# Order of the last products in the odd channels of the core stage, and the count of two kinds of tiles

## The chip, the cores and the metric

The kernel runs on one NeuronCore of a Trainium2 chip. The metric is the device time of one execution in microseconds. Five engines work side by side from queues of their own: PE (matrix products, with its weight loads shown apart as PEld), DVE (vector), ACT (scalar), POOL (GpSimd) and SP (which here issues the transfers). An instruction that needs another engine's result waits at the head of its own queue, and what stands behind it waits too.

## What is computed

Two layers on a pair tensor x of 384 x 384 tokens with 128 channels. Only the first one bears on the change:

```python
z = _layernorm(x, norm_g, norm_b)
left = (z @ Wl + bl) * sigmoid(z @ Wlg + blg)
right = (z @ Wr + br) * sigmoid(z @ Wrg + brg)
core = einsum('bikh,bjkh->bijh', left, right)     # for each of 128 channels h: 384x384 times 384x384
zo = _layernorm(core, onorm_g, onorm_b) @ Wout + bout
x = x + sigmoid(x @ Wg + bg) * zo
```

The second layer makes left, right and gate from the new x, multiplies left by the row sum of right and by the gate, goes through one more matrix and normalises over the channels.

## The kernel before, in words

There are three stages, one after the other. **Stage 1** (0 to about 1010 us) reads x, makes `left` and `right` and writes them to `lr_d` in device memory, ordered by channel. **Stage 2** (about 1010 to 1746 us) makes the core, channel by channel, and writes it to `core_d`. **Stage 3** (to the end) reads the core back row by row and does everything else. The change lies in stage 2.

Stage 2 is the loop of line 664 over channels h, 126 of them, and a short ending for the last two (lines 720 to 769). For each channel `load_h` (L92) brings left and right together into a tile `lrh` of three that take turns. ACT copies the right half to a tile `rr` of its own (`apart`, L632), of the pool `p2r` with three buffers: three copies for each channel, one for each block of 128 summands. The result goes to a tile `ct` of the pool `p2out` with two buffers, from which SP stores it (`store_core`, L645). Line 718 asks for the load of channel h+3 at the end of channel h, when its tile is free again.

Channels go in pairs, and the two passes of a pair differ.

**Even channel** (lines 668 to 682): `plain` computes the product in nine block products of 384 columns, three for each of three banks of `pc`. Beside it POOL prepares the odd channel: `left_sums` (L618, four small sums into `ss`) and `right_sums2` (L623, L627, L628, into `tt`), both in the tile `arena` but for one piece.

**Odd channel** (lines 684 to 716): the upper two thirds of the product are made with seven products per two-by-two block, instead of eight, in the manner of Strassen and Winograd. The block row 2 is plain: three products of 384 columns into bank `b4`. Eleven products of 192 columns go into banks `b0` to `b3`. DVE combines them in eight additions (`add`, L651). Their order on PE and DVE is written out by hand, since every instruction is given through `seq`, which keeps the order of the program on its engine. The part that matters:

```python
add(base, b1, one)            # L702
add(more2, b2, base)          # L703
add(base, b3, base)           # L704
add(least, b2, base)          # L705: the fourth sum, the last reader of b2
product(b0, ...); product(b0, ...); product(b1, ...); product(b1, ...)   # L706 to L709
product(b2, block(h, 2, 1), B[2][1])                                    # L710
product(b3, ...); product(b3, ...)                                      # L711, L712
```

A bank is read by DVE in the first four additions and is then written by PE once more, in the products of L706 to L712, so each of those products has to wait for the last addition that read its bank. `b0` is read by ACT (L692), `b1` by L702, `b3` by L704, and `b2` by L703 and L705. All products have one helper line, L648: in the profile those of the even pass have the name `pc` and those of the odd one the name `b`. Each product of float32 shows as two weight loads and two matmuls.

Also on the way: `squares` (L635, ACT) and `add_sum` and `add_squares` (L638 and L642, DVE) gather the sums for the normalisation; `stay` (L610, POOL) copies the part of left and right that never left the chip; at the end `fill` (L585 to L592, POOL) does for channel 127 what ACT does for the others.

Of the kernel before, what the change touches and what calls it, by code (L numbers as in the profile page):

```python
# [19 lines left out]
def triangle_then_gated_row_kernel(ctx: ExitStack, tc: tile.TileContext, a: dict, out: bass.AP):  # L20
# [35 lines left out]
    def seq(ins):  # L56

        return tc.keep_in_program_order(ins)
# [21 lines left out]
    with ExitStack() as ctx2:  # L80
# [4 lines left out]
        def load_h(h):  # L85

            if h < H:
                t = inp[h % 3 // 2].tile([P, NB, N, 2], F32, tag="lrh", name="lrh")
                src = lr_d[:, :, h].rearrange("g p e -> p g e")
                dst = t.rearrange("p b (g i) s -> p (b g) (i s)", i=G)  # L90
                for g in slice(0, NG), slice(NG, NB * NG - KEEP):
                    seq(nc.sync.dma_start(out=dst[:, g], in_=src[:, g]))  # L92
                loaded2[h] = t
# [465 lines left out]
            seq(nc.vector.scalar_tensor_tensor(r, r, -0.5, ve, ALU.mult, ALU.mult))  # L559
            seq(nc.vector.scalar_tensor_tensor(r, r, 1.5, m, ALU.add, ALU.mult))  # L560

        with tc.tile_pool(name="p2r", bufs=3, side="right", reuse_waits="tile") as rrp, \
             tc.tile_pool(name="p2more", bufs=1, side="right", reuse_waits="tile") as more, \
             tc.tile_pool(name="p2out", bufs=2, side="right", reuse_waits="tile") as op, \
             tc.tile_pool(name="p2st", bufs=1, side="right", reuse_waits="tile") as stp:
            csum = spool.tile([P, NB, N], F32, name="csum")
            csq = spool.tile([P, NB, N], F32, name="csq")
# [5 lines left out]
            right = {}  # L573
# [23 lines left out]
            js = slice(0, J), slice(J, N)  # L597
            one, base, more2, least = (arena[:, n, j] for n in (2, 2 * NB) for j in js)
# [5 lines left out]
            def block(h, k, i):  # L604
                return loaded2[h][:, k, i * P:(i + 1) * P, 0]

            def stay(h):

                for (kb, ig), lrt in kept.items():
                    seq(nc.gpsimd.tensor_copy(loaded2[h][:, kb, ig * G:(ig + 1) * G], lrt[:, h]))  # L610

            def left_sums(h):

                for n, x, y, op in ((0, block(h, 0, 1), block(h, 0, 0), ALU.subtract),
                                    (1, block(h, 0, 1), block(h, 1, 1), ALU.add),
                                    (2, ss[1], block(h, 0, 0), ALU.subtract),
                                    (3, block(h, 1, 0), ss[2], ALU.subtract)):
                    seq(nc.gpsimd.tensor_tensor(ss[n], x, y, op))  # L618

            def right_sums2(h):  # L620

                rr = right[h]
                seq(nc.gpsimd.tensor_tensor(  # L623
                    tt[:, 0:2], rr[:, 0, js[1]].unsqueeze(1).to_broadcast([P, 2, J]),
                    rr.rearrange("p b n -> p (b n)").rearrange("p (a m) -> p a m", a=2)[:, :, js[0]], ALU.subtract,
                ))
                seq(nc.gpsimd.tensor_tensor(tt[:, 2], rr[:, 0, js[0]], tt[:, 1], ALU.subtract))  # L627
                seq(nc.gpsimd.tensor_tensor(tt[:, 3], rr[:, 1, js[0]], tt[:, 2], ALU.subtract))  # L628

            def apart(h, k):  # L630

                seq(nc.scalar.copy(right[h][:, k], loaded2[h][:, k, :, 1]))  # L632

            def squares(h):
                seq(nc.scalar.activation(sq, cts[h], AF.Square))  # L635

            def add_sum(h, c=None):
                seq(nc.vector.tensor_add(csum, c or cts[h], csum))  # L638

            def add_squares(h):  # L640
                if h >= 0:
                    seq(nc.vector.tensor_add(csq, csq, sq))  # L642

            def store_core(h, queue=nc.sync):
                seq(queue.dma_start(out=core_d[:, h, :].rearrange("(b p) j -> p b j", p=P), in_=cts[h]))  # L645

            def product(to, lhsT, rhs, start=True, stop=True):
                seq(nc.tensor.matmul(to, lhsT=lhsT, rhs=rhs, start=start, stop=stop))  # L648

            def add(out, ps, term):  # L650
                seq(nc.vector.tensor_add(out, ps, term))  # L651

            def plain(h, banks):

                for k in range(NB):
                    for i in range(NB):
                        product(banks[i], block(h, k, i), right[h][:, k], k == 0, k == NB - 1)

            fill(0)
            with tc.tile_pool(name="p2mix", bufs=1, space=PSUM, reuse_waits="tile") as mps:  # L660
                pc = mps.tile([P, NB, 512], F32, name="pc")
                b0, b1, b2, b3 = (mps.tile([P, 512], F32, name="b%d" % n)[:, :J] for n in range(4))
                b4 = mps.tile([P, 512], F32, name="b4")[:, :N]
                for h in range(H - 2):
                    cts[h] = op.tile([P, NB, N], F32, tag="ct", name="ct")
                    right[h + 1] = rrp.tile([P, NB, N], F32, tag="rr", name="rr")
                    if h % 2 == 0:
                        plain(h, [pc[:, i, :N] for i in range(NB)])
                        if h > 0:
                            store_core(h - 1)  # L670
                        add_squares(h - 2)
                        stay(h + 1)
                        left_sums(h + 1)
                        for k in range(NB - 1):
                            apart(h + 1, k)
                        right_sums2(h + 1)
                        if h > 0:
                            squares(h - 1)
                            add_sum(h - 1)
                        apart(h + 1, NB - 1)  # L680
                        if h > 0:
                            add_squares(h - 1)
                    else:
                        rr, ct = right[h], cts[h]
                        B = [[rr[:, k, j] for j in js] for k in range(NB)]
                        product(b0, block(h, 0, 0), B[0][0])
                        for k in range(NB):
                            product(b4, block(h, k, 2), rr[:, k], k == 0, k == NB - 1)
                        seq(nc.scalar.copy(cts[h - 1], pc[:, :, :N]))
                        store_core(h - 1)  # L690
                        add_sum(h - 1, pc[:, :, :N])
                        seq(nc.scalar.copy(one, b0))  # L692
                        stay(h + 1)
                        for k in range(NB - 1):
                            apart(h + 1, k)
                        seq(nc.scalar.copy(ct[:, 2], b4))
                        apart(h + 1, NB - 1)
                        squares(h - 1)
                        product(b1, ss[2], tt[:, 2])
                        product(b2, ss[0], tt[:, 1])  # L700
                        product(b3, ss[1], tt[:, 0])
# [3 lines that stand above are left out]
                        add(least, b2, base)  # L705
                        product(b0, block(h, 1, 0), B[1][0], True, False)  # L706
                        product(b0, block(h, 2, 0), B[2][0], False, True)
                        product(b1, ss[3], B[1][1], True, False)
                        product(b1, block(h, 2, 0), B[2][1], False, True)  # L709
                        product(b2, block(h, 2, 1), B[2][1])  # L710
                        product(b3, block(h, 1, 1), tt[:, 3], True, False)  # L711
                        product(b3, block(h, 2, 1), B[2][0], False, True)  # L712
                        add(ct[:, 0, js[0]], b0, one)
                        add(ct[:, 0, js[1]], b1, base)
                        add(ct[:, 1, js[1]], b2, least)
                        add(ct[:, 1, js[0]], b3, more2)
                    del right[h], loaded2[h]
                    load_h(h + 3)
                store_core(h)
            with tc.tile_pool(name="p2ps", bufs=2, space=PSUM, reuse_waits="tile") as ps, \  # L720
                 tc.tile_pool(name="p2one", bufs=1, space=PSUM, reuse_waits="tile") as ps1:
                for h in range(H - 2, H):
# [19 lines left out]
                    ct = op.tile([P, NB, N], F32, tag="ct", name="ct")  # L742
# [32 lines left out]
    with ExitStack() as ctx3:  # L775
        def pool(name, bufs, **kw):
            return ctx3.enter_context(tc.tile_pool(name=name, bufs=bufs, reuse_waits="tile", **kw))
# [3 lines left out]
        wp, sp, op, up = pool("p3w", 4), pool("p3s", 4), pool("p3out", 3), pool("p3u", 18)  # L781
# [324 lines left out]
```

## Time and profile before

| what | value |
|---|---|
| median of 3 runs | 3151.19 us (3149.53 to 3152.18) |
| the profiled execution's own time | 3148.3 us |
| its span | 3146.2 us |
| granted PE clock | 0.999 |
| PE busy | 3126.9 us (99%) |
| PE idle between matmuls in 1030 to 1730 us | 0.48 us of 700 us |
| DMA share in 1030 to 1380 and 1380 to 1730 us | 0.97 and 0.96, at 286 GB/s |

The span is the time from the first instruction to the last in the one execution that was profiled, and lies 2.1 us under that execution's own time. A matmul's end is modelled in these profiles, and matmuls overlap one another, so a PE that counts as busy can still be held up: the starts of the instructions tell more than the busy time does. A view of the trace merges neighbouring instructions of one kind; "x4" at the end of a line is their number, and what stands in brackets after it is the idle time of the engine before the first of them and who ended it.

### The profile page before, as it was taken

How to read it: one execution, taken by the hardware profiler on the slowest of the kernel's cores; microseconds unless marked ns; L12 is line 12 of the kernel's file. 1: busy time of each engine (PE TensorE's matmuls, PEld its weight loads, DVE VectorE, ACT ScalarE, POOL GpSimd, SP SyncE). 2: the span in 40 equal slices, each digit the busy share in tenths (PEclk: the TensorE clock that was granted, in tenths of full speed). 3: DMA queues.
4: the chain of work that ended last, by engine and by line, in shares of the span. 5: the costliest groups of instructions: out<-in, count | busy, mean ns of one | idle time of the engine just before them, and what ended most of it. 6: DMA issues, size and time to landing. Idle time of an engine off the chain costs nothing.

```text
span 3146.2 us, 47062 instructions
## 1 busy us (share of the span) xinstructions
PE 3126.9 (99%) x11936; PEld 2208.3 (70%) x11936; DVE 2586.9 (82%) x7913; ACT 1947.3 (62%) x4196; POOL 2380.6 (76%) x3003
## 2 busy tenths in 40 slices
PE   9999999999999999999999999999999999999998
PEld 4777777777777777777777666677777777777776
DVE  8888888888886777776777888888888888888998
ACT  4444444444444555555655577677777777777776
POOL 6888888888886666656666588788888888888887
PEclk9999999999999999999999999999999999999999
DMA  4988878788883999999999865666666666666562
GB/s 153 339 302 306 323 281 339 280 324 302 302 316 99 284 287 287 284 287 286 284 288 285 289 230 209 224 225 218 223 216 221 217 222 218 219 221 220 207 216 106
DMA packets 509117, 797.58 MB, mean 254 GB/s; under 512 B 56689, under 2 KB 419569, under 8 KB 492466
## 3 DMA queue, kind: packets, MB, share of 16 engines
q1 hardware_dynamic: 507952, 793.20, 74.3%
q8 instruction: 99, 1.62, 0.2%
q14 instruction: 168, 1.38, 0.1%
q10 hardware_dynamic: 834, 1.18, 0.1%
q0 software_dynamic: 64, 0.20, 0.0%
HBM read 508.14 MB, written 286.36 MB: 253 GB/s over the span
## 4 chain that ended last, share of the span: by engine, by line
PE 98%; DVE 1%; ACT 0%; issue 0%; POOL 0%; POOLq 0%; DVEq 0%; ACTq 0%
PE pr L372 31%; PE pc L648 12%; PE b L648 11%; PE py L904 8%; PE pr L875 8%; PE pg L892 8%; PE pl L893 8%; PE pg L844 8%; PE py L905 4%; PE pt L335 0%; PE pc L732 0%; PE pq L852 0%; ACT py L939 0%; PE pb L863 0%; POOL rs L286 0%
## 5 line engine op out<-in xcount | busy, mean ns | idle before, releaser
L372 PE MATMUL pr<-wz,xc 128*128 128x512 f32 x2176 | 934.7, 592 | 0.0
L372 PEld LDWEIGHTS pr<-wz,xc 128*128 128x128 f32 x2176 | 670.5, 308 | 263.4 <-POOL xc L324 0.8
L383 ACT ACTIVATE sg<-pr,rs 128x256 f32<-128x256 f32 x1152 | 483.7, 471 | 508.1 <-ACT sg L383 354.8
L385 DVE SCALAR_TENSOR_TENSOR lr<-pr,rs,sg 128x256 f32<-128x256 f32 x1152 | 502.3, 478 | 163.9 <-ACT sg L383 158.6
L939 ACT ACTIVATE py<-py,nm,rs 128x128 f32<-128x128 f32 x1149 | 493.2, 430 | 159.2 <-DVE u L897 81.6
L904 PEld LDWEIGHTS py<-wo,u 128*128 128x128 f32 x2304 | 376.6, 191 | 97.5
L904 PE MATMUL py<-wo,u 128*128 128x128 f32 x2304 | 402.1, 275 | 0.0
L866 POOL TENSOR_TENSOR cs<-ct,rt 128x384 f32<-128x384 f32 x380 | 378.6, 997 | 8.2 <-PE pr L875 3.3
L974 POOL TENSOR_TENSOR yt<-yt,lnb 128x384 f32<-128x384 f32 x380 | 379.6, 1000 | 2.9 <-DVE yt L968 2.8
L648 PE MATMUL pc<-rr,lrh 128*128 128x384 f32 x1134 | 376.1, 486 | 1.1 <-POOL rr L591 1.1
L324 POOL TENSOR_TENSOR xc<-xc,bc 128x512 f32<-128x512 f32 x272 | 345.3, 1270 | 24.0
L286 POOL TENSOR_TENSOR rs<-nd,mhalf 128x8 f32<-128x8 f32 (+1 forms) x145 | 236.3, 1630 | 147.1 <-ACT sg L383 109.2
L919 DVE BATCH_NORM_STATS2 st<-py 128x6 f32<-128x128 f32 x1152 | 266.5, 287 | 87.8 <-PE py L905 86.0
L905 PE MATMUL py<-ident,x1T 128*128 128x128 f32 x1152 | 314.0, 273 | 0.0
L875 PE MATMUL pr<-cs,wc 128*128 128x384 f32 x768 | 313.5, 490 | 0.0
L892 PE MATMUL pg<-x1T,mat_L_conv_W_gate 128*128 128x384 f32 x768 | 310.7, 486 | 0.9 <-ACT g L895 0.9
L844 PE MATMUL pg<-xt,mat_L_conv_Wg 128*128 128x384 f32 x768 | 310.7, 487 | 0.3 <-ACT ct L758 0.2
L648 PEld LDWEIGHTS pc<-rr,lrh 128*128 128x128 f32 x1134 | 220.3, 196 | 129.1 <-POOL rr L591 1.8
L893 PE MATMUL pl<-x1T,mat_L_conv_W_left 128*128 128x384 f32 x768 | 310.5, 486 | 0.0
L618 POOL TENSOR_TENSOR arena<-lrh 128x128 f32<-128x128 f32 x126 | 110.5, 877 | 256.6 <-DMA lrh<-lr_d 211.7
L648 PE MATMUL b<-rr,lrh 128*128 128x192 f32 x1134 | 296.5, 386 | 0.5 <-DVE arena L651 0.5
L895 ACT ACTIVATE g<-pg,col_L_conv_b_gate 128x384 f32<-128x384 f32 x384 | 223.0, 581 | 103.4 <-PE pg L892 92.8
(151 smaller groups left out, 5209.3 us busy)
## 6 DMA issues: line engine op xcount, KB each, us to landing
lr_d<-lr SPq DMA_DIRECT2D x128, 1024.0 KB
lrh<-lr_d SPq DMA_DIRECT2D x128, 640.0 KB
xt<-in_x_row_dram SPq DMA_DIRECT2D x96, 768.0 KB
ct<-core_d SPq DMA_DIRECT2D x95, 768.0 KB
rt<-rstd_d SPq DMA_DIRECT2D x95, 768.0 KB
core_d<-ct SPq DMA_DIRECT2D x126, 576.0 KB
out_dram<-yt SPq DMA_DIRECT2D x94, 768.0 KB
xt<-in_x_nat_dram SPq DMA_DIRECT2D x136, 512.0 KB
```

What stands on the lines that cost most here:

```text
L372: seq(nc.tensor.matmul(pr[:, r, :], lhsT=columns[n][:, 4 * q + i, :] if n < PLAIN else columns[n][:, q, :, i], rhs=wz, start=True, stop=Tr ...
L383: seq(nc.scalar.activation(sg[r], pr[:, r, 2 * H:], AF.Sigmoid, scale=rs[r]))
L385: seq(nc.vector.scalar_tensor_tensor(t[:, :, c * XR + r0 + r, :], pr[:, r, :2 * H].rearrange("k (h s) -> k h s", s=2), rs[r], sg[r].rearra ...
L648: seq(nc.tensor.matmul(to, lhsT=lhsT, rhs=rhs, start=start, stop=stop))
L844: seq(nc.tensor.matmul(pg[:, :N], lhsT=wg0, rhs=r["xT"], start=True, stop=True))
L875: seq(nc.tensor.matmul(pr[:, :N], lhsT=wc, rhs=r["cs"], start=True, stop=True))
L892: seq(nc.tensor.matmul(pg2[:, :N], lhsT=wgate, rhs=r["x1T"], start=True, stop=True))
L893: seq(nc.tensor.matmul(pl[:, :N], lhsT=wleft, rhs=r["x1T"], start=True, stop=True))
L904: seq(nc.tensor.matmul(py[:, s], lhsT=r["u"][:, s], rhs=r["wo"], start=True, stop=False))
L905: seq(nc.tensor.matmul(py[:, s], lhsT=r["x1T"][:, s], rhs=ident, start=False, stop=True, is_transpose=True))
L939: seq(nc.scalar.activation(py[:, s], py[:, s], AF.Identity, bias=bias, scale=scale))
L974: seq(engine.tensor_tensor(yt, yt, lnbb, ALU.add))
```

## The change

In the odd pass, the product into `b2` (L710) goes behind the two into `b3` (L711, L712), and the two additions that read them at the end (L715, L716) change places in the same way. The pool `p2r` (tiles `rr`) has two buffers in place of three, and `p2out` (tiles `ct`) three in place of two; both kinds have the same size, so the two pools together take the same room. Nothing is computed otherwise.

```diff
-        with tc.tile_pool(name="p2r", bufs=3, side="right", reuse_waits="tile") as rrp, \
+        with tc.tile_pool(name="p2r", bufs=2, side="right", reuse_waits="tile") as rrp, \
              tc.tile_pool(name="p2more", bufs=1, side="right", reuse_waits="tile") as more, \
-             tc.tile_pool(name="p2out", bufs=2, side="right", reuse_waits="tile") as op, \
+             tc.tile_pool(name="p2out", bufs=3, side="right", reuse_waits="tile") as op, \
              tc.tile_pool(name="p2st", bufs=1, side="right", reuse_waits="tile") as stp:
...
                         product(b1, block(h, 2, 0), B[2][1], False, True)
-                        product(b2, block(h, 2, 1), B[2][1])
                         product(b3, block(h, 1, 1), tt[:, 3], True, False)
                         product(b3, block(h, 2, 1), B[2][0], False, True)
+                        product(b2, block(h, 2, 1), B[2][1])
                         add(ct[:, 0, js[0]], b0, one)
                         add(ct[:, 0, js[1]], b1, base)
+                        add(ct[:, 1, js[0]], b3, more2)
                         add(ct[:, 1, js[1]], b2, least)
-                        add(ct[:, 1, js[0]], b3, more2)
```

## The prediction

> **What bounds the kernel now.** I read the busy times and the chain of the page first, then the stage by windows, then the waits of the product line, then single stretches of the timeline.
>
> ```profile
> PE 3126.9 (99%) x11936; PEld 2208.3 (70%) x11936; DVE 2586.9 (82%) x7913; ACT 1947.3 (62%) x4196; POOL 2380.6 (76%) x3003
> ...
> PE 98%; DVE 1%; ACT 0%; issue 0%; POOL 0%; POOLq 0%; DVEq 0%; ACTq 0%
> ```
>
> PE is the chain almost throughout, so only what holds PE counts. But "99%" doesn't say that PE is never held: ends of matmuls are modelled. In the view of line 648:
>
> ```profile
> its engine sat idle before it (us, times) until:
>   DVE arena L651: 12.4, 65
>   POOL rr L591: 2.9, 2
>   POOL arena L627: 0.5, 2
> ```
>
> The product line waits for a DVE addition into `arena` 65 times, nearly once in each of 63 pairs of channels. The timeline of PE and of its weight loads in one pair says where:
>
> ```profile
> 1513.60 0.81 PE L648 MATMUL b<-rr,lrh 128*128 128x192 f32 x4
> 1514.25 0.49 PE L648 MATMUL b<-rr,s 128*128 128x192 f32 x2
> 1514.57 0.97 PE L648 MATMUL b<-rr,lrh 128*128 128x192 f32 x4
> 1515.38 0.49 PE L648 MATMUL b<-arena,lrh 128*128 128x192 f32 x2
> 1515.71 0.49 PE L648 MATMUL b<-rr,lrh 128*128 128x192 f32 x2
> ```
>
> ```profile
> 1514.41 0.36 PEld L648 LDWEIGHTS b<-rr,lrh 128*128 128x128 f32 x2
> 1514.95 0.31 PEld L648 LDWEIGHTS b<-rr,lrh 128*128 128x128 f32 x2 [0.17 <-DVE arena L651]
> ```
>
> The first column is the start. Four matmuls take 0.65 us from start to start (1513.60 to 1514.25), but the four from 1514.57 take 0.81: 0.16 us lost, between the second product of `b1` (L709) and that of `b2` (L710). The weight load of L710 waits for the fourth addition (L705, `least`). DVE's timeline shows its four additions:
>
> ```profile
> 1513.22 1.67 DVE L651 TENSOR_TENSOR arena<-b,arena 128x192 f32<-128x192 f32 x4
> ```
>
> They end at 1514.89, and the weight load starts at 1514.95. From all starts of the trace: a matmul of 192 columns follows another after 162.5 ns and one of 384 after 322.5, everywhere in the stage, but for two places around L710 (215 and 275 ns). That is 165 ns in each of 61 pairs; in two pairs the third and fourth additions are 350 ns late, and 515 ns are lost. A pair takes 11.48 us.
>
> **What the Trainium skill says.** PSUM — Partial Sum Buffer, "PSUM bank collisions raise a hardware error": two engines may not be on one bank at once, reads with reads included, so PE must wait for the reader of the bank. The trace agrees: L710's load starts 0.06 us after `least` ends. TensorE: Matmul & The Clock Gate, "Step-by-step: what each phase is for": matmuls stay in program order and only weight loads are pulled ahead. So PE can't pass L710, though L711 and L712 could run; the trace shows them behind it. SBUF — State Buffer, on the two separate sides of access (engine ports and DMA): DVE with two SBUF inputs and POOL lock each other out of a port pair for a whole instruction. Here L618 takes 458 ns at the least and 1456 at the median for one form; this matters for the first rival. Perfetto Trace Analysis, "Identifying the Most-Contended Engine": occupancy of 16 DMA engines is misleading; here it is 0.96 to 0.97 in this stage.
>
> **Part 1, the order of products.** Removed: L710's wait. The two `b3` products (four matmuls) come first, and `b3` was last read by the third addition (L704). In a usual pair, counted from the first `pc` matmul, L704 ends at 9.94 us and `least` at 10.34. The weight load at this place would start at 10.18 without a wait; releases take 0.05 us more. So `b3` is free 0.18 us early, and `b2`, now 4 x 162.5 = 650 ns later (10.83), 0.44 us early. Both waits go. `tt[:, 3]` (L628), which L711 needs too, is over two us earlier. Gain: 61 x 165 ns + 2 x 515 ns = 11.1 us. In the two odd pairs the third addition ends at 10.30; released at 10.35, the load is 0.17 us late. A load put off by 0.21 us (10.39 for 10.18) cost PE 0.165, so this costs some 0.12: 2 x 0.12 = 0.25 us stay. On DVE the eight additions are the same; the last one still follows PE's last product, and its bank isn't written again for six us. Nothing else is moved, no DMA among it.
>
> **Part 2, three `ct` tiles.** A `ct` waits for the store three channels back, not two. In the waits of 1030 to 1760 us:
>
> ```profile
> POOL arena L618 <- DMA lrh<-lr_d: 209.6, 97, 4.0
> ...
> ACT rr L632 <- DMA lrh<-lr_d: 106.6, 77, 3.3
> ACT ct L696 <- DMA core_d<-ct: 27.0, 33, 1.8
> ```
>
> The 27.0 us should go. Behind L696 on ACT stand the third copy to `rr`, `squares`, and the next pass's copies. PE needs the third copy for the next even pass's seventh product (after 12 matmuls of 322.5 ns, 3.9 us into it), and it is there before; nothing of the 27 us reaches PE. Worth 0; it keeps SP's late stores harmless.
>
> **Part 3, two `rr` tiles.** A wait is added: the first copy for the next odd channel must now wait until PE has read the odd channel before it. ACT in the pair shown:
>
> ```profile
> 1515.62 0.53 ACT L632 COPY rr<-lrh 128x384 f32<-128x384 f32 x1
> 1517.79 0.55 ACT L632 COPY rr<-lrh 128x384 f32<-128x384 f32 x1 [1.64 <-DMA lrh<-lr_d]
> ```
>
> The copy at 1515.62 would start when the last odd matmul ends, about 1516.25, and end by 1516.8. Queued behind it on ACT is the copy of 1517.79, which waits for its load anyway, and `squares` behind that. Cover: 1 us here, and over 0.4 in nearly every pair (second copies start at 1.25 us or later in most). PE needs the first copy 5.5 us into the even pass, POOL's L623 needs it about 5.5 us in. Without the cover it would cost ACT up to 0.6 us, still not PE. In the odd pass the copies stand behind L689, which has waited for the even pass already. Cost 0. At the end, `fill` of channel 127 now waits for channel 125's products (1734.5, not 1731.5), but its next step waits for a load until 1736.15 anyhow, with 0.7 us of small copies to do: 0. The two pools keep their room together; which tiles of stage 3 lie over which is shifted by one tile, taken as 0, at most 1 us either way.
>
> **What is late next.** The loads. DMA's share leaves 0.035 of 11.48 us. Work of 0.965 x 11.48 = 11.08 us would be 97.9% of the new pair, 24 x 322.5 + 22 x 162.5 ns = 11.315 us. It fits, barely. The odd channel's load is asked for when the even pass before it ends, so its deadline comes 165 ns sooner. On it hang L618, L623, L627, then the first product that uses `tt` (L699). From the end of L627 to that weight load there are 0.57 us in the typical pair, but 52, 53, 67 and 113 ns in four, and under 300 in seven; two already wait (0.26 us). If all shift by 165 ns, the four lose 0.11 + 0.11 + 0.10 + 0.05 = 0.4 us; by twice that (load delayed as well), seven lose 1.3. I take 1.0; bounds 0 and, if the DMA share can't rise at all, the whole 11. I take little because stretches of 0.6 us in the transfers' view of two pairs reach 366 to 381 GB/s against a mean of 286, so the share isn't a wall.
>
> **Sum.** -11.1 + 0.25 + 1.0 = -9.8 us. Against the profiled execution: 3148.3 - 9.8 = 3138.5 (span 3136.4). The median of the runs is 2.9 us above that execution: 3151.2 - 9.8 = 3141.4. That median's runs differ by 2.7 us; some 0.2% (6.3 us) is what a measurement can tell from no change.
>
> **Rivals.** *Loads take part of it* (0.14): the chain load, L618, L627, L699 stalls PE in a third or more of the pairs. For it: 209.6 us of POOL's waits are for loads, and a first L618 that starts after DVE's L642 is locked out and loses over a microsecond. Against: typical slack 0.57 us, and each stall gives the loads time again. 21 to 42 pairs at 0.17 us: 3.5 to 7 us off the 10.85 us, 3144 to 3147.5. *The wait moves* (0.07): the release for `b3` is counted at the fourth addition, or the third comes later than now; then the change doesn't do what it says and L711 waits where L710 did: 3151. For: slack is only 0.18 us. Against: in 61 pairs that addition's end varies by under 20 ns. *Two `rr` tiles bind, slower* (0.06): if the copy for the next odd channel must wait for the even pass under way (its nine products end at 6.0 us), the first two copies run from 6.0 to 7.1, L623 to 8.1, L627 to 8.7, against a weight load at 7.74: 1.0 us in 63 pairs, 63 - 11 = 52 us slower, 3203. It decides from the point where copies end after some 5.5 us. Against: the tile is taken from the channel two back, which PE has left at 0.2 us.
>
> **How the numbers follow.** Forecast 0.73, its own range 3139 to 3143.5; loads 0.14; moved wait 0.07; slower 0.06. The range 3138.5 to 3147 takes in the forecast and most of the loads' case. Faster by over 0.2% (under 3144.9): 0.73 + 0.04 = 0.77; within 0.2%: 0.10 + 0.07 = 0.17; slower 0.06.
>
> **What would show it.** Right: 162.5 ns from start to start all through the odd pass, 11.315 us for a pair, L648's idle time for DVE near 0, no wait of L696 for a store, first `rr` copies at about 0.2 us into the even pass. Wrong: waits of L648 for POOL L627 in many pairs (loads), for DVE L651 at L711 (moved), or for ACT L632 (two tiles).

## The result, and the profile after

The changed kernel takes 3137.5 us (median of 5 runs, 3136.1 to 3139.4), the kernel before 3151.1 in the same comparison (5 runs, 3149.5 to 3152.2): ratio 0.9958, 95% interval 0.9943 to 0.9972, or 13.6 us less. The forecast was 3141.4, range 3138.5 to 3147.0: the direction was right, the gain was larger than the range allowed, by 1 us. Two later comparisons gave 11.9 and 12.0 us.

The profiled execution of the changed kernel took 3139.4 us, span 3137.6. The view of line 648, in which the kernel before had waited 65 times for a DVE addition:

```profile
its engine sat idle before it (us, times) until:
  issue: 1.4, 3
  POOL arena L627: 1.0, 3
  DVE lr L385: 0.4, 1
```

The wait for `arena` from DVE's line 651 is gone. DVE's L385 and most of "issue" belong to the start of the stage; POOL's L627 will matter below. PE's timeline in one pair (first column start, then length, and the number of instructions at the end of the line):

```profile
1497.18 0.81 PE L648 MATMUL b<-rr,lrh 128*128 128x192 f32 x4
1497.83 0.49 PE L648 MATMUL b<-rr,s 128*128 128x192 f32 x2
1498.15 0.49 PE L648 MATMUL b<-rr,lrh 128*128 128x192 f32 x2
1498.48 0.49 PE L648 MATMUL b<-arena,lrh 128*128 128x192 f32 x2
1498.80 0.81 PE L648 MATMUL b<-rr,lrh 128*128 128x192 f32 x4
1499.45 4.03 PE L648 MATMUL pc<-rr,lrh 128*128 128x384 f32 x12
```

From 1497.18 to 1499.45 there are 14 matmuls in 2.27 us, 162 ns each: no gap is left. The fourth line is the first `b3` product, which now stands where the `b2` product waited. A pair takes 11.315 us from start to start, to the nanosecond what the forecast gave, where it was 11.48. And the waits of the stage (engine and line, what it waited for, us in all, times, the longest):

```profile
ACT rr L632 <- DMA lrh<-lr_d: 108.1, 86, 2.9
...
ACT rr L632 <- PE b L648: 60.1, 54, 1.4
...
POOL rr L586 <- PE b L648: 3.1, 1, 3.1
...
PEld b L648 <- POOL arena L627: 1.0, 3, 0.6
```

The copies to `rr` now wait 60.1 us for PE, the price of two tiles; the first copy of a pair starts at 0.2 us of it, as forecast, and ends at 0.75 us in nearly every pair. Nobody waits for them. The wait of L696 for a store (27.0 us before) is gone.

Below, a profiled execution is split by PE's first matmuls: stage 1 up to the first product of the core; "the pairs", from there to the first product of channel 126; and the rest. All "excess" times are sums over the starts of matmuls in the 63 pairs, each beyond 162.5 or 322.5 ns.

| us | stage 1 | the pairs | rest |
|---|---|---|---|
| before | 1010.5 | 724.0 | 1411.7 |
| after | 1012.4 | 713.6 | 1411.7 |

The pairs give 10.4 us; stage 1, which the change doesn't touch but for its end, went the other way by 1.9 in this one execution. So the trace of one execution showed less than the medians, and the question was what the rest is.

### The profile page after: what moved, and what is told of

Its sections match the earlier page's. It is cut to its first block, busy times and chain, and to the rows that moved or that the text cites. A ratio compares the mean times of both kernels' runs of the same rounds, so it can differ in the third digit from the quotient of the medians.

```text
span 3137.6 us, 47186 instructions
## 1 busy us (share of the span) xinstructions
PE 3117.4 (99%) x11936; PEld 2209.1 (70%) x11936; DVE 2581.1 (82%) x7913; ACT 1949.7 (62%) x4196; POOL 2369.4 (76%) x3003
## 4 chain that ended last, share of the span: by engine, by line
PE 98%; DVE 1%; ACT 0%; POOL 0%; issue 0%; DMA 0%; SPq 0%; POOLq 0%; DVEq 0%; ACTq 0%
PE pr L372 31%; PE pc L648 12%; PE b L648 11%; PE py L904 8%; PE pr L875 8%; PE pg L892 8%; PE pl L893 8%; PE pg L844 8%; PE py L905 4%; PE pc L732 0%; DMA stage<-in_x_nat_dram 0%; PE pq L852 0%; PE pt L335 0%; POOL rs L286 0%; DVE lr L385 0%
## 5 line engine op out<-in xcount | busy, mean ns | idle before, releaser
L385 DVE SCALAR_TENSOR_TENSOR lr<-pr,rs,sg 128x256 f32<-128x256 f32 x1152 | 501.9, 477 | 165.6 <-ACT sg L383 160.1
L632 ACT COPY rr<-lrh 128x384 f32<-128x384 f32 x378 | 205.0, 553 | 171.5 <-DMA lrh<-lr_d 108.4
L618 POOL TENSOR_TENSOR arena<-lrh 128x128 f32<-128x128 f32 x126 | 105.4, 837 | 259.4 <-DMA lrh<-lr_d 206.4
```

The lines of the kernel that those rows point to most:

```text
L385: seq(nc.vector.scalar_tensor_tensor(t[:, :, c * XR + r0 + r, :], pr[:, r, :2 * H].rearrange("k (h s) -> k h s", s=2), rs[r], sg[r].rearra ...
```

## The experiments

My theory at the start: the order of the products brings everything, the tiles nothing. The rivals: the tiles bring the 3 us that were left over; or shorter pairs can't do without the third `ct` tile. In every table, "lost before tt" is the excess at the first product that uses `tt` (L699), that is, PE waiting for POOL's L627; "late L642" counts pairs whose first addition L642 starts after 0.6 us of the pair, where 0.48 is usual.

**The kernel before and the changed one again.**

> The kernel before, unchanged, to see how far stages 1 and 3 alone differ from run to run. Theory (the whole gain is the wait of the b2 product): its 63 pairs take 724.0 us again; stage 1 lies anywhere between 1008 and 1013 us, ratio 1.000 within 0.001. Rival (the kernel after has a second gain of some 3 us outside the pairs): stage 1 and stage 3 repeat within 0.5 us here, so that a difference of 3 us means something.

> The changed kernel, unchanged, a second time. Theory: the 63 pairs take 713.6 us again, 10.4 less than before, and the ratio is 0.9967, 3140.7 for 3151.1; what went beyond that in the first measurement (13.6 us of median) was spread of stages 1 and 3. Rival (a second gain outside the pairs): 13.6 us less again, ratio 0.9957, and stage 1 or stage 3 shorter by 3 us in the trace.

Measured: the kernel before had ratio 1.0003 (0.9995 to 1.0011) to 26 other runs of itself in that comparison, whose median was 3149.21; the changed kernel 0.9963 (0.9950 to 0.9975), 3137.33 us, 11.9 us less, between the theory's 0.9967 and the rival's 0.9957. Its level is that of the first time; it is the kernel before that was 1.9 us lower here. The traces: pairs at 713.62 for the changed kernel, as expected, but 725.80 for the kernel before, not 724.0. Stage 1 was 1010.6 and 1010.3. In the view of line 648 of the kernel before, second time:

```profile
  DVE arena L651: 12.2, 65
  POOL arena L627: 4.4, 6
  POOL rr L591: 2.9, 2
```

L627 had been 0.5 us in the profile that the forecast was made from. So the kernel before has a second loss, which happened to be nearly absent in that one profile.

**One half at a time.** The order alone takes the changed kernel and gives it back the tiles:

```diff
-        with tc.tile_pool(name="p2r", bufs=2, side="right", reuse_waits="tile") as rrp, \
+        with tc.tile_pool(name="p2r", bufs=3, side="right", reuse_waits="tile") as rrp, \
-             tc.tile_pool(name="p2out", bufs=3, side="right", reuse_waits="tile") as op, \
+             tc.tile_pool(name="p2out", bufs=2, side="right", reuse_waits="tile") as op, \
```

The tiles alone are the other lines of the change: two `rr`, three `ct`, products and additions in the order of before.

> Only the products and additions change places; three rr tiles and two ct tiles as before. Theory: all of the gain, pairs at 713.6 us, ratio 0.9967; ACT again waits some 27 us for stores before L696 and no rr copy waits for PE. Rival 1 (the tiles bring a part): pairs above 715 us or a ratio 3 us worse than the full change. Rival 2 (shorter pairs need the third ct tile): stores hold ACT longer, over 40 us, and the pairs come to 717 us or more.

> Only the counts of tiles change, two rr and three ct; order of products as before. Theory: no change, pairs at 724.0 us within 0.5, ratio 1.000; the wait of L696 for stores is gone and rr copies wait some 60 us for PE instead, both off the path. Rival 1 (the tiles bring the 3 us): ratio 0.999 and a stage that is shorter by 3 us. Rival (two rr tiles cost): pairs over 725 us.

Measured: the order alone 0.9968 (0.9957 to 0.9980), 3138.95 us, 10.3 less; pairs at 714.13, L696 waits 32.7 us for stores. The tiles alone 0.9998 (0.9989 to 1.0006), 3148.30 us; pairs at 724.24, excess at the two places of L710 10.9 us (11.05 in the kernel before). So the order brings nearly all, and the full change, in the same comparison, is 1.6 us under the order alone. The traces showed where to look. In the order alone PE lost 0.8 us before `tt`, in three pairs, each with a late L642; in one of them, ACT, DVE, POOL and the weight loads:

```profile
1248.86 0.48 ACT L696 COPY ct<-b 128x384 f32<-128x384 f32 x1 [1.02 <-DMA core_d<-ct]
1249.23 0.55 ACT L632 COPY rr<-lrh 128x384 f32<-128x384 f32 x1
1249.67 1.17 ACT L635 ACTIVATE arena<-ct 128x1152 f32<-128x1152 f32 x1
```

```profile
1250.87 1.36 DVE L642 TENSOR_TENSOR csq<-csq,arena 128x1152 f32<-128x1152 f32 x1 [0.88 <-ACT arena L635]
1252.15 1.35 DVE L638 TENSOR_TENSOR csum<-ct,csum 128x1152 f32<-128x1152 f32 x1
1254.47 1.36 DVE L642 TENSOR_TENSOR csq<-csq,arena 128x1152 f32<-128x1152 f32 x1 [0.97 <-ACT arena L635]
```

```profile
1252.93 0.94 POOL L618 TENSOR_TENSOR arena<-lrh 128x128 f32<-128x128 f32 x1 [2.29 <-DMA lrh<-lr_d]
1253.95 0.46 POOL L618 TENSOR_TENSOR arena<-arena,lrh 128x128 f32<-128x128 f32 x1
1254.49 1.66 POOL L618 TENSOR_TENSOR s<-lrh,arena 128x128 f32<-128x128 f32 x1
```

```profile
1257.83 0.79 PEld L648 LDWEIGHTS b<-arena 128*128 128x128 f32 x5 [0.81 <-POOL arena L627]
```

Read it downwards. A store still holds the `ct` tile, so L696 waits 1.02 us. Behind it on ACT stands `squares` (L635), which therefore ends at 1250.84. DVE's L642 needs it and starts at 1250.87, which is 1.47 us into the pair in place of 0.48. That pushes DVE's three long additions back; the last of them, at 1254.47, coincides with the fourth L618, which takes 1.66 us where 0.46 is its time alone. In this pair the load was late too (2.29 us). L627 ends late, and the weight load of L699 waits 0.81 us. With three `ct` tiles the first link is missing. The link from DVE to POOL is the one the Trainium skill describes (SBUF — State Buffer, section "SBUF: two separate sides"): a DVE instruction with two SBUF inputs, as L642 and L638 here, and a POOL instruction that reads SBUF exclude each other, each for its whole length. The trace agrees: 1.66 us beside L642, 0.46 us alone.

**Is the link real?** Three edits of the new order. First, two tiles of each kind: only the third `ct` tile is missing.

```diff
-             tc.tile_pool(name="p2out", bufs=3, side="right", reuse_waits="tile") as op, \
+             tc.tile_pool(name="p2out", bufs=2, side="right", reuse_waits="tile") as op, \
```

> The new order with two rr tiles and two ct tiles, so that of the change only the third ct tile is missing. Theory now (two rr tiles cost nothing; the third ct tile takes away some stalls at the first product with tt, since no store then delays squares on ACT and with it the addition L642 on DVE, which shuts POOL out): as the new order alone, pairs at 713.8 to 715 us, L696 waits for stores 25 to 40 us, PE waits for L627 in 3 to 10 pairs, ratio 0.9968. Rival (the two rr tiles bring what the full change has beyond the order): pairs under 713.7 us and hardly a wait for L627.

Measured: 0.9967 (0.9955 to 0.9980), 3138.09 us; pairs at 714.61, L696 waits 25.3 us for stores, 1.3 us lost before `tt` in two pairs, L642 late in both (1.69 and 1.90 us). Weight loads wait five times for L627; PE loses time in two of these pairs. As the theory said; two `rr` tiles don't take this loss away. The time tells less than the profile: 3138.09 us is 11.9 us under the kernel before of this comparison, as far as the full change came in two others.

Second, with three `rr` and two `ct` tiles, `squares` ahead of the copy that waits for the store:

```diff
+                        squares(h - 1)
                         seq(nc.scalar.copy(ct[:, 2], b4))
                         apart(h + 1, NB - 1)
-                        squares(h - 1)
```

> The new order, three rr and two ct tiles, and in the odd pass squares goes ahead of the copy L696 on ACT, so that a store which holds L696 no longer holds squares. Theory (the link from the store to PE is squares, L642, POOL): L696 still waits for stores, but L642 starts at 0.48 us of nearly every even pass, and the stalls for L627 are as with three ct tiles, 0 to 2 pairs and under 0.4 us lost; ratio 0.9963 to 0.9965. Rival (stores delay the loads themselves, or the link is the copies to rr): waits for L627 in 3 to 10 pairs as with the order alone, ratio 0.9968.

Measured: 0.9968 (0.9955 to 0.9980), 3139.50 us; pairs at 714.31, 0.8 us lost before `tt` in two pairs. L642 was late in one pair of 62, against 15 and 6 in two profiles of the order alone, so that link was cut nearly as meant. But the expectation failed: the ratio is the rival's, and the loss was not smaller than with the order alone (0.8, and 0.4 in its second profile). One of the two pairs that lost time had a late load instead, with the second L618 at 3.76 us; the other is the one with the late L642 (1.24 us). The copy of L696, line 697 here, waited for stores only three times, 2.8 us in all: `squares` covers most of that wait. With two such pairs the run decides nothing.

Third, the opposite: the changed kernel with L642 late in every pair. No load, store or product moves; what moves is `squares` on ACT, and with it the second copy to `rr`, which now stands behind it.

```diff
-                        add_squares(h - 2)
                         stay(h + 1)
                         left_sums(h + 1)
-                        for k in range(NB - 1):
-                            apart(h + 1, k)
+                        apart(h + 1, 0)
+                        if h > 0:
+                            squares(h - 2)
+                        add_squares(h - 2)
+                        apart(h + 1, 1)
...
                         apart(h + 1, NB - 1)
-                        squares(h - 1)
                         product(b1, ss[2], tt[:, 2])
...
                     if h == H - 2:
+                        squares(h - 2)
                         add_squares(h - 2)
```

> The changed kernel with one thing made late on purpose: the squares of the even channel go behind the first rr copy of the next even pass on ACT (which waits for PE until 0.2 us), so that the addition L642 starts at 1.95 us of every even pass instead of 0.48, as it did in single pairs behind a store. No load, store or product is moved. Theory (a late L642 is what shuts POOL out and stalls the first product with tt): waits of PE for L627 in most of the 63 pairs, 0.3 to 0.8 us each, pairs at 730 to 765 us, ratio 1.001 to 1.012. Rival (the stalls come from late loads, and L642 is late beside them): a handful of waits as before, pairs at 713.5 to 716 us, ratio 0.9963 to 0.997.

Measured: 1.0027 (1.0018 to 1.0036), 3160.09 us, by the ratios some 20 us over the changed kernel. L642 starts at 1.89 us at the median, pairs take 733.5 us, and of 20.6 us excess 20.2 lie before `tt`. In the waits of the stage:

```profile
DVE csq L642 <- ACT arena L635: 87.0, 63, 2.4
...
PEld b L648 <- POOL arena L627: 39.9, 59, 1.9
```

A late L642 alone is enough: 59 weight loads wait for L627, where the changed kernel has 1 to 6 in its four profiles. The second copy to `rr` is not what holds POOL: in each of the 63 pairs L623 starts at the end of the fourth L618 and at least 1.2 us after that copy. In the pair from 1105.68 us on, the last three L618 take 1.56, 1.45 and 1.46 us. This is the link from L642 to PE, shown by itself. Its size came out at the low end of what I expected, 0.3 us a pair, because POOL gets in between DVE's additions where the load is early.

**How often it happens by itself.** Four more profiles.

> The new order alone a second time, for its stalls: the first time three pairs lost 0.8 us in all before the first product with tt. Theory (late L642 behind stores): again 2 to 5 such pairs, each with L642 at over 1.1 us of the pair, pairs at 713.8 to 715 us. Rival (chance of the loads alone): such pairs have L642 at 0.48 us.

> The kernel before a third time, for its pairs: 724.0 and 725.8 us so far. Theory (stalls of L627 behind a held store come and go): 724 to 726 us, with 0 to 2 us lost at the first product with tt. Rival (the 725.8 was an exception): 724.0 again within 0.2.

> The changed kernel a third time, for its pairs: 713.57 and 713.62 so far. Theory (with three ct tiles no store holds squares, L642 is never late): 713.4 to 713.8 us and L642 at 0.48 us in all pairs. Rival (chance): over 714 us, as with the order alone.

> The tiles alone a second time, for its pairs: 724.2 us so far, with 0.4 us lost at the first product with tt in one pair. Theory: 723.9 to 724.4 us, L642 never late. Rival (chance): 725 us or more.

Measured: pairs at 713.75 (order alone), 727.98 (before), 715.09 (after), 723.95 (tiles alone). The single times of these runs were 3139.45, 3158.04, 3140.17 and 3148.62 us; the second of them has a stage 1 of 1015.6 us, 5 more than the first profile of the same kernel, and its 4.1 us lost before `tt` are beyond the 0 to 2 that I expected. My expectation for the changed kernel failed too: 1.8 us were lost before `tt`, with L642 at 0.48 us in all pairs. The loads alone did it, the second L618 starting at 4.80 us in one pair and 3.97 in the other. The one for the order alone held half: of its two pairs one had a late L642. All profiles of the unedited halves, with the three that follow under "The halves once more":

| profiles | lost before tt, us | pairs held up by over 20 ns | of these with late L642 |
|---|---|---|---|
| two ct: before (3), order alone (3), two and two (1) | 0, 1.9, 4.1; 0.8, 0.4, 2.4; 1.3 | 20 | 18 |
| three ct: after (4), tiles alone (3) | 0.3, 0.3, 1.8, 0.6; 0.4, 0.1, 0.4 | 10 | 0 |

Means: 1.6 and 0.5 us. One of the 18 is a pair of the kernel before with L642 at 0.69 us and the second L618 as late as 4.63 us: there the load is the cause, of 1.15 of that profile's 1.9 us.

In most of these pairs the load is late beside L642, so the rival that loads do it all has to be answered. In 16 of the 18 the second L618 starts 1.26 to 1.41 us after L642, and ACT's second copy, 0.11 us before it, shows that the load has just landed. The pairs of these 14 profiles can be compared at equal loads, by the start of that copy, which waits for its load in all the pairs counted below. With L642 on time, no pair is held in which the copy starts before 3.4 us; the twelve that are held have it at 3.43 to 4.69 us. With L642 at 1.2 us or later and the copy at 2.5 to 3.2 us, all 13 pairs are held, 5.3 us in all, and of the 136 pairs with L642 on time and the copy in the same stretch not one. So the loss has two sources, a late L642 and a late load, and the third `ct` tile takes the first away: L642 is late in 5 to 15 pairs of a profile with two `ct` tiles, and in none with three (the first pair, where nothing has been stored yet, left out). The size of it, about 1 us by the means, is less certain: one execution, long as a whole (3158.04 us), gives 4.1 us of it, and without it the means are 0.6 us apart.

**A lost wait made longer.** The order of before, but with the `b2` product earlier, ahead of the two into `b1`:

```diff
                         product(b0, block(h, 2, 0), B[2][0], False, True)
+                        product(b2, block(h, 2, 1), B[2][1])
                         product(b1, ss[3], B[1][1], True, False)
                         product(b1, block(h, 2, 0), B[2][1], False, True)
-                        product(b2, block(h, 2, 1), B[2][1])
```

> The order of before, but with the b2 product moved the other way, ahead of the two into b1. Its weight load would then be due at 9.53 us of the pair, and the fourth addition still releases the bank at 10.39: 0.86 us late where the kernel before is 0.21 us late for 0.165 us of PE. Theory (PE is held by this release and by nothing else here, and a late load costs its lateness less 0.04 us): 0.82 us lost in each pair, 0.65 more than before, pairs at 724.0 + 41 = 765 us, ratio 1.013. Rival (the lost 0.165 us was a fixed price of one waiting instruction, not the lateness): 0.165 us again, ratio 1.000.

Measured: 1.0130 (1.0114 to 1.0145), 3190.27 us; pairs at 764.8, 0.81 us lost in a usual pair. Both numbers are the theory's. It is the lateness of the release that PE pays, and the place in the order that sets it. The two additions that change places with the products were not tested apart; L642, which stands behind them, starts at 0.48 us of a usual pair before and after.

**The halves once more, on one chip.**

> The changed kernel timed a third time. Theory (the order is worth 10.7 us, the third ct tile about 1 more, and the 13.6 us of the first measurement held some 2 us of a high level of the kernel before): 11 to 12.5 us less, ratio 0.9961 to 0.9965. Rival (the first measurement was the usual size): 13.6 us again, ratio 0.9957.

> The new order alone, timed on the same chip as the full change. Theory: some 1 us above the full change, 0.5 to 1.6, as in the first comparison (3138.95 against 3137.33), stalls for L627 with L642 late in 2 to 5 pairs. Rival (the tiles are worth nothing): within 0.4 us of the full change.

> The tiles alone, timed on the same chip. Theory: 0.5 to 2 us under the kernel before, ratio 0.9993 to 0.9998, L642 never late. Rival (worth nothing): ratio 1.000 or over.

Measured: the full change 0.9961 (0.9948 to 0.9973), 3137.43 us, 12.0 less than 3149.46; the order alone 0.9967 (0.9955 to 0.9979), 3139.78 us; the tiles alone 0.9998 (0.9989 to 1.0006), 3148.76 us. The full change is 2.35 us under the order alone (1.6 the first time), more than the 0.5 to 1.6 expected; the tiles alone are 0.7 under the kernel before (0.9 the first time). The ratio of the tiles alone doesn't clear its interval, so their size rests on the traces. Pairs: 713.87, 715.68 and 724.32.

These traces showed a second effect of the tiles, at the passage from stage 1 to stage 2, where `fill` makes the first `rr`. POOL's timeline of the kernel before:

```profile
1009.57 0.87 POOL L591 COPY rr<-lrh 128x768 f32<-128x768 f32 x1 [17.86 <-PE pr L372]
```

and what the view of line 591 says of the changed kernel:

```profile
L591 POOL COPY rr<-lrh x2: 882/1446/2009, 1005.2 to 1729.1; 128x768 f32<-128x768 f32 x2
...
  PE pr L372: 10.8, 1
```

The copy waits for the last reader of what lay at that place in stage 1. It starts 0.75 us after the start of stage 1's last matmul in all eight profiles with three `rr` tiles, and 6.2 us before it in all nine with two. The first product of the core follows that matmul after 1.67 us in the eight (1.665 to 1.675), and after 0.96 to 1.05 in the nine: 0.7 us, which is not in the numbers for the pairs. That the place of the first tile moved is read from the code; that the gain goes with the count of `rr` tiles is shown.

## Why the prediction was right in kind and too small

The step that failed is in the sum, not in the wait that the change removes. The loads were put at +1.0 us, counted from a loss of 0, and the tiles at 0. At the product with `tt`, where both act, the runs show about -1.0 us on the mean, and the place of the tiles gave -0.7 more. Term by term:

**The wait of L710.** Right. Forecast 11.1 us removed and 0.25 left in the two odd pairs; measured 11.05 removed and 0.37 left (0.18 in each of them, where 0.12 was forecast; the second of the two gaps there was not thought of). That is 10.7 us. The order alone gave 10.3 and 9.7 in the medians. That `b3` would be free in time, though by 0.18 us only, held in 61 pairs.

**"Nothing of the 27 us reaches PE. Worth 0" (three `ct` tiles).** Wrong. I followed what stands behind L696 on ACT as far as the copies and `squares`, and looked only at when PE needs the copies. `squares` has a reader too, L642 on DVE, and DVE and POOL shut each other out; from there the way to PE is the very chain (L618, L627, L699) that I priced two paragraphs later for the loads. Measured: about 1 us on the mean of the profiles. The medians are not of one mind: past the 0.7 us of the passage, the full change beats the order alone by 0.9 and 1.65 us, but the tiles alone beat the kernel before by 0.2 us at most, and two sets of runs of one kernel differ by 0.6 in the median (3149.21 and 3149.84). That there is such a gain is shown; its size is not.

**The place of tiles, "taken as 0, at most 1 us either way".** The bound held, the sign was there to be found: I looked for the tiles of stage 3 that come to lie over these, and not for those of stage 1 that lay there before. Measured: 0.7 us.

**The loads, +1.0 us.** Measured in the four profiles of the changed kernel: 0.3, 0.3, 1.8 and 0.6, so 0.7 on the mean. The size was about right; but it was counted from a base of 0, the one profile of before. That kernel loses 0, 1.9 and 4.1 us at the same place in its three profiles. Shorter pairs add no loss that these runs can show: the tiles alone, with the longer pair, lose 0.1 to 0.4.

**From the profiled execution to the median.** The step that cost most. The forecast put the gain of one execution, 9.8 us, under a median that lay 2.9 us above that execution, as if the 2.9 were untouched by the change. Part of them is likely to be just this loss before `tt`, which that one profile lacks; the runs without a profile can't show it. With the runs' numbers the sum is -10.7 - 0.7 - 1.0 = -12.4 us, which fits the 11.9 and 12.0 of the later comparisons and lies within the interval of the first (9 to 18 us). Why the kernel before stood at 3151.1 in the first comparison and at 3149.2 and 3149.5 in those two (3150.0 and 3150.9 in the two others), with the changed kernel at 3137.3 to 3137.5 in all three, stays open; a gain of 12.0 us from the forecast's 3151.2 would have been 3139.2, within its range. As to other parts of the kernel, stage 1, the same in all kernels but for its end, ran from 1009.4 to 1015.6 us in the profiles.

**Two `rr` tiles.** Right on the path that was costed: the copies wait 60 us for PE, and the tiles alone cost nothing. `fill` at the end waited 3.1 us for PE (L586, in the waits above), and the rest of the kernel stayed at 1411.7 us. The rivals "the wait moves" and "two tiles bind" didn't occur, nor did the loads hold 21 pairs or more: one or two of 63 in each profile of the changed kernel.

**The range.** Its low end, 3138.5, is what was forecast for the profiled execution, and lies 1.85 us under 3151.2 less the 10.85 us of the removed wait. The gain of the third `ct` tile was taken as 0, and the up to 1 us for the place of the tiles was not put into the range either.

## What to carry to other kernels

Where a bank has several readers, write last the one whose last reader ends last: what PE pays is the lateness of the release at the place where the product stands, so an independent product moved between costs nothing and hides it. When a wait goes that "nobody waits for", follow everything queued behind it to its readers on the other engines, and through the port pair of DVE and POOL, before calling it free. And one profile of before may lack a loss that the usual execution has: take a second look at a term that varies from pair to pair before the gain of one execution is carried over to a median.

## What the runs showed of the hardware that was not expected

The spacing of float32 matmuls is so regular that a loss of 165 ns in 11.48 us is read without doubt: 162.5 ns for 192 columns and 322.5 for 384, in every pair of every profile, but for the waits named above. A weight load that waits costs PE its lateness less about 0.05 us: 0.21 us late cost 0.165, and 0.86 late cost 0.81. A DVE addition over 1152 columns with two inputs in SBUF stretches POOL's 0.46 us addition to 1.66 in the pair shown, and to as much as 1.69 in the other profiles.
